# The first product of layer 1 in seven-product form over pairs of super-tiles, with a planned order

## The chip, the cores and the metric

One core of a Trainium2 chip (trn2) runs the whole kernel. The metric is device time in microseconds (us): 1892.49 us is the median of 8 runs before the change (1891.74 to 1893.44), lower is better. The engines are called PE (TensorE), DVE (VectorE), ACT (ScalarE), POOL (GpSimd) and SP (the queue that issues most DMAs). Each takes its instructions in program order.

## The reference

Four residual layers over `x` of 128 graphs x 64 nodes x 256 features, all in float32. Each layer adds to `x` what a different graph block makes of `h = relu(layernorm(x))`. Layer 0 is two graph convolutions followed by four LSTM passes over windows of 1 to 4 nodes; layer 2 weights three parts of the adjacency; layer 3 is masked attention. The change is in layer 1, which is:

```python
h = jnp.maximum(_layernorm(x, axis=-1), 0.0)
agg = jnp.einsum('nm,bmd->bnd', A_hat, h)             # A_hat: normalised adjacency, 64 x 64
z = agg.reshape(-1, d) @ W1.T + b1                    # the first product: 256 -> 512
h = jax.nn.relu(_batchnorm(z, g1, be1))               # statistics over all 8192 rows
out = _batchnorm(h @ W2.T + b2, g2, be2)              # the second product: 512 -> 256
x = x + out.reshape(b, n, -1)
```

Because of the first batchnorm, all 8192 rows of `z` must exist before the second product can start.

## The kernel before

The 8192 rows are cut into 16 super-tiles of 512 rows (`NS` = 16, `SUP` = 512), each of four blocks of 128 rows (`Q` = 4). Features are held in chunks of 128 partitions: 2 for 256 features (`KC`), 4 for 512 (`HC`). The kernel goes through its stages in order: the graph convolutions (about the first 200 us), the LSTM passes (to about 1217 us), the first product of layer 1 (to about 1364 us), its second product, then layers 2 and 3.

There is no automatic scheduler. In most stages the order on each engine is written by hand: a step is noted with a planned time by `at(t, fn, ...)`, the notes are sorted by that time, and the instructions are issued in the sorted order. The times decide the order alone; the waits between engines come from semaphores. The first product alone is issued in another way: `first_product` is a generator that stops at each `yield`, and `pipelined` takes the next piece of several generators in turn.

What one super-tile s goes through in `first_product`: its `x` is loaded into `xt`; `to_token_major` turns the LSTM result `hT` with eight PE transposes (L229), and DVE adds the two halves onto `xt` (L230); `xt` is stored to `x1d`; `norm_of` makes the layernorm figures on DVE (L193 to L197), with one power on POOL (L196); `normalize_relu` makes `h` on ACT (L203); `aggregate` multiplies with `ahT` on PE (L219, eight products of 128 columns) and DVE copies the two banks into `ag` (L220); then for each of the four output chunks two products of 128x512 (L522) go into one bank, which ACT moves with its bias to `zslot(s, o)` (L524). At last DVE takes the statistics of the four chunks (L527), and `bn_coeffs` turns the statistics of all super-tiles into the coefficients `co1` (L761 to L767), two chunks at a time.

In the trace every matmul of this float32 kernel leaves two PE records, so the 128 products of L522 are 256 records.

The first three super-tiles are begun while the LSTM's last steps still run: `begin` puts pieces of `first_product` into the LSTM's plan. The last LSTM steps contain, in this order of dependence, the gate sums on DVE (L628), gate activations on ACT (L624), the cell updates on POOL (L651), their tanh on ACT (L656) and the last states on DVE, written into `hT` (L576). DVE also makes the sums `tx` for the LSTM's own seven-product form (L568). All PSUM tiles come from one pool of eight banks (`bank`).

The LSTM, the second graph convolution, the second product and a product of layer 3 are already in seven-product form. There a 2x2 block of products (two input chunks by two output chunks, over two row blocks) is done with seven products in place of eight, at the price of sums of weights, sums of inputs, and adds of results. The names are those of the code:

```python
    A11, A12, A21, A22, S1, S2, S4 = range(7)
    S3 = A21
    OF = (None, A11, A12, S4, A22, S1, S2, S3)
```

`weight_sum(w, k)` makes the weight sums S1 to S4 on POOL. `adj3` and `smask` are constants used in layers 2 and 3, made in `adjacency_parts` near the start of the kernel.

## Time and profile before

| | us |
|---|---|
| median of 8 runs | 1892.49 |
| lowest and highest run | 1891.74, 1893.44 |
| the profiled execution's own time | 1891.74 |
| its span, first to last instruction | 1889.9 |
| granted TensorE clock | 1.000 |

How the page and the answers are read: a row of the first part gives an engine's busy time, its share of the span and its number of instructions. A row of the chain of waits gives start, duration and the work that the end of the kernel hung on at that time. A row of the table by stretch gives from:to, its length, then busy time and number of instructions of PE, PE's weight loads (PEld), DVE, ACT and POOL, the granted clock, the DMA share and GB/s. A row of the timeline gives start, duration, engine, line, operation, what it writes and reads, the number of instructions merged, and in brackets how long the engine was idle before it and what ended that. Where rows are merged, the duration covers all of them.

The busiest groups of the first product's stage, from the groups of instructions: L522 on PE 112.3 us in 256 records, L219 31.2 us, L229 17.0 us; L524 on ACT takes 0.67 to 0.69 us for one, L527 on DVE 0.68.

### The profile page before, as it was taken

What the parts mean: (1) busy time and instruction counts of PE and PEld (TensorE: products, weight loads), DVE (VectorE), ACT (ScalarE), POOL (GpSimd) and SP (SyncE); (2) the same over time, 40 slices, a digit from 0 to 9 for tenths busy, and PEclk for the clock granted to TensorE, in tenths of its full rate; (3) what the DMA queues carried; (4) which work ended last, traced back from release to release, by engine and by line L of the source; (5) the groups of instructions that cost most, each with busy time, mean ns of one, the idle gap of its engine ahead of it and who ended that gap; (6) DMA issues with size and microseconds to landing.
All of it is one profiled execution on the core that took longest, in us unless ns stands there. A gap on an engine that the chain in (4) does not pass through costs nothing.

```text
span 1889.9 us, 19675 instructions
## 1 busy us (share of the span) xinstructions
PE 1866.6 (99%) x7112; PEld 1176.6 (62%) x7112; DVE 1127.7 (60%) x2264; ACT 892.2 (47%) x1539; POOL 577.2 (31%) x459
## 2 busy tenths in 40 slices
PE   8999999999999999999999999999999999999999
PEld 7996444444445666665444444565444788888887
DVE  6775777635446345435633333577787776677774
ACT  6775766534435435434533333444475344433442
POOL 4441422533325432422532222311053312211220
PEclk9999999999999999999999999999999999999999
DMA  4110001000001000000000000233200111111100
GB/s 139 57 57 0 1 1 42 3 1 0 1 0 45 1 0 1 1 0 23 0 0 1 1 0 23 89 108 108 83 1 1 45 45 43 37 45 45 46 23 34
DMA packets 49537, 54.32 MB, mean 29 GB/s; under 512 B 3104, under 2 KB 44832, under 8 KB 49440
## 3 DMA queue, kind: packets, MB, share of 16 engines
q1 hardware_dynamic: 48976, 52.87, 8.9%
q8 instruction: 56, 0.92, 0.2%
q10 hardware_dynamic: 464, 0.20, 0.1%
q14 instruction: 41, 0.34, 0.1%
HBM read 36.28 MB, written 16.78 MB: 28 GB/s over the span
## 4 chain that ended last, share of the span: by engine, by line
PE 95%; DVE 3%; ACT 1%; POOL 1%; issue 0%; DMA 0%; SPq 0%; DVEq 0%; POOLq 0%
PE ps L606 34%; PE ps L612 19%; PE ps L1012 8%; PE ps L522 6%; PE ps L842 5%; PE ps L338 3%; PE ps L348 3%; PE ps L1076 3%; PE ps L377 2%; PE ps L1052 2%; PE ps L1000 2%; PE ps L1086 2%; PE ps L219 2%; PE ps L1117 1%; PE ps L229 1%; PE ps L1025 1%
## 5 line engine op out<-in xcount | busy, mean ns | idle before, releaser
L628 DVE TENSOR_TENSOR gate<-gate,ps 128x512 f32<-128x512 f32 (+2 forms) x378 | 224.0, 620 | 448.3 <-PE ps L612 369.0
L606 PE MATMUL ps<-tx,wih 128*128 128x512 f32 (+2 forms) x1008 | 446.8, 542 | 2.7 <-ACT gate L631 1.0
L606 PE MATMUL ps<-hT,wih 128*128 128x512 f32 (+2 forms) x756 | 338.5, 541 | 0.0
L631 ACT COPY gate<-ps 128x512 f32<-128x512 f32 (+2 forms) x252 | 134.5, 534 | 378.1 <-PE ps L612 325.0
L606 PEld LDWEIGHTS ps<-tx,wih 128*128 128x128 f32 x1008 | 190.5, 190 | 193.0 <-issue 130.6
L624 ACT ACTIVATE gate<-gate,lbias 128x512 f32<-128x512 f32 (+2 forms) x252 | 216.7, 860 | 157.9 <-DVE gate L628 157.9
L612 PE MATMUL ps<-h,whh 128*128 128x512 f32 (+2 forms) x576 | 256.6, 527 | 0.0
L606 PEld LDWEIGHTS ps<-hT,wih 128*128 128x128 f32 x756 | 143.6, 190 | 141.6 <-issue 79.4
L612 PE MATMUL ps<-th,whh 128*128 128x512 f32 (+2 forms) x432 | 192.5, 527 | 0.0
L1012 PE MATMUL ps<-wl,ag 128*128 128x256 f32 x768 | 172.1, 380 | 0.0
L612 PEld LDWEIGHTS ps<-h,whh 128*128 128x128 f32 x576 | 109.4, 190 | 100.2 <-issue 76.5
L651 POOL TENSOR_TENSOR gate<-gate 128x1024 f32<-128x1024 f32 (+2 forms) x36 | 71.9, 2019 | 306.7 <-ACT gate L624 306.7
L1012 PEld LDWEIGHTS ps<-wl,ag 128*128 128x128 f32 x768 | 143.4, 190 | 20.2 <-ACT ag L1005 1.8
L651 POOL TENSOR_TENSOR cell<-gate 128x1024 f32<-128x1024 f32 (+2 forms) x36 | 79.4, 2228 | 175.2 <-ACT gate L624 175.2
L612 PEld LDWEIGHTS ps<-th,whh 128*128 128x128 f32 x432 | 82.1, 190 | 75.2 <-issue 57.4
L968 POOL TENSOR_TENSOR ln_rn<-ln_rn,mhalf 128x4 f32<-128x4 f32 (+1 forms) x33 | 32.8, 994 | 300.7 <-DVE ln_rn L967 300.2
L975 ACT ACTIVATE h<-x,ln_rn 128x256 f32<-128x256 f32 x128 | 68.3, 594 | 103.1 <-DVE ln_rn L971 103.1
L522 PE MATMUL ps<-ag,w 128*128 128x512 f32 x256 | 112.3, 592 | 0.0
L651 POOL TENSOR_TENSOR cell<-gate,cell 128x1024 f32<-128x1024 f32 (+2 forms) x32 | 65.2, 2055 | 109.3 <-ACT gate L624 109.3
L631 DVE COPY gate<-ps 128x512 f32<-128x512 f32 (+2 forms) x126 | 78.6, 624 | 20.8 <-PE ps L612 20.8
L656 ACT ACTIVATE gate<-cell 128x1024 f32<-128x1024 f32 (+2 forms) x72 | 68.1, 951 | 29.6 <-POOL cell L651 29.6
L522 PEld LDWEIGHTS ps<-ag,w 128*128 128x128 f32 x256 | 47.6, 190 | 54.5 <-issue 50.9
(212 smaller groups left out, 2800.3 us busy)
## 6 DMA issues: line engine op xcount, KB each, us to landing
xt<-in_x_dram SPq DMA_DIRECT2D x30, 512.0 KB, 4.4
x1d<-xt SPq DMA_DIRECT2D x16, 512.0 KB, 2.9
x<-x1d SPq DMA_DIRECT2D x16, 512.0 KB, 5.1
out_dram<-x SPq DMA_DIRECT2D x15, 512.0 KB, 3.4
wih<-in_WihT_dram SPq DMA_DIRECT2D x16, 256.0 KB, 5.4
whh<-in_WhhT_dram SPq DMA_DIRECT2D x12, 256.0 KB, 5.4
xt<-in_x_dram SPq DMA_DIRECT2D x8, 128.0 KB, 3.6
wl<-in_W_dram SPq DMA_DIRECT2D x3, 256.0 KB, 3.0
```

Source lines behind the costliest of these rows:

```text
L338: nc.tensor.matmul(p_[:, ts(q, P)], v[h][:, q, ts(c, P)], adjT_bd, start=True, stop=True)
L522: nc.tensor.matmul(p_, con["w1"][:, c, ts(o, P)], ag[:, c, :], start=(c == 0), stop=(c == KC - 1))
L606: nc.tensor.matmul(wide(p_[:, :N]), wih[0][:, OF[k], gi, :], x_, start=first_, stop=(j == 0), skip_group_check=True)
L612: nc.tensor.matmul(p_[:, :N], whh[0][:, OF[k], gi, :], h_, start=False, stop=True, skip_group_check=True)
L624: nc.scalar.activation(to, r[bank_][:, :N] if bank_ else to, fn, bias=lbias[:, l, m : m + 1])
L628: nc.vector.tensor_add(slot(n, hc), slot(n, hc), r[bank_][:, :N])
L631: op(slot(n, hc), r[bank_][:, :N])
L651: fn(*((t["G"] if isinstance(t, dict) and "G" in t else st["c"])[:, n, :, : st["N"]] for t in tiles))
L656: nc.scalar.activation(o_, c, AF.Tanh)
L842: nc.tensor.matmul(banks[name], w2[:, OF[j], k, :], x_, start=(new and k == 0), stop=(k == 1), skip_group_check=True)
L975: nc.scalar.activation(v[tag][:, q, :], v[src][:, q, :], AF.Relu, bias=v["rn"][:, 1, q : q + 1], scale=v["rn"][:, 0, q : q + 1])
L1012: nc.tensor.matmul(v["W"][:, q, :], v["ag"][:, c, m, ts(2 * k + q, P)], wl2[m][:, c, :], start=(n == 0), stop=(n == 3 * KC - 1))
```

## The change

The first product gets the seven-product form, over pairs of super-tiles and pairs of output chunks: for each pair `i` of super-tiles and each half `g` of the 512 outputs, `half(i, g)` issues seven products of 128x512, which collect in three banks named a, b and c. Bank a takes four products, and is read after each of them; b takes two and is read after each; c takes one. A read is an eviction with bias on ACT (`evict`) or an add onto `z` on DVE (`add`). The fourth product of bank a is issued in the next half.

The generator is replaced by a class `First`, whose steps are issued from a planned list with a period of `GATE` = 8.7 for each half. In it the turned LSTM result is copied from PSUM to `h` by ACT and added onto `xt` by POOL (`turned`, `added`), POOL multiplies the layernorm shift (`root`), and ACT copies the aggregated banks to `ag` (`agged`). The three sums T1, T2, T4 of inputs, and a fourth made in place of `b12`, are `ag_sums`: on POOL, except for the first and the last pair, which have them on DVE. Four super-tiles are begun in the LSTM's last steps, a fifth is loaded there.

PSUM pools are now opened and closed by `new_banks`: eight banks as one pool, but in the first product's loop five for its products ("gates") and three for turns and aggregations ("rest"). The sums of the LSTM's second state, of layer 1 and of layer 3 share one tile (`sums_of`). `adj3` and `smask` are made in a passing tile `parts`, stored to DRAM, and loaded again after the first product; `w1` lies in another pool, with four loads and with weight sums on POOL; the weight sums of `w2` move to the front of the loop.

```diff
-    psum = ctx.enter_context(tc.tile_pool(name="psum", bufs=8, space=bass.MemoryType.PSUM))
...
     graph_weights, first = other_end("first", 1)
-    def bank():
-        return psum.tile([P, 512], F32, tag="ps", name="ps")
+    banks = {}
+    def new_banks(**n):
+        for scope, _ in reversed(list(banks.values())):
+            scope.close()
+        banks.clear()
+        for name, bufs in n.items():
+            scope = ExitStack()
+            banks[name] = scope, scope.enter_context(tc.tile_pool(
+                name=name, bufs=bufs, space=bass.MemoryType.PSUM, reuse_waits="tile"))
+    def bank(pool="psum"):
+        return banks[pool][1].tile([P, 512], F32, tag="ps", name="ps")
+    new_banks(psum=8)
...
-        con["w1"] = weight("w1", a["W1T"])
+        con["w1"] = hlast.tile([P, 7, 2, P], F32, tag="w1", name="w1")
+        for o in range(2):
+            for c in range(2):
+                nc.sync.dma_start(con["w1"][:, 2 * o + c], a["W1T"].rearrange(
...
-    adj3 = const.tile([P, 3, P], F32, tag="adj3", name="adj3")
-    smask = const.tile([P, P], F32, tag="smask", name="smask")
+    parts = first.tile([P, 4, P], F32, tag="parts", name="parts")
+    parts_d = dram.tile([P, 4, P], F32, tag="parts_d", name="parts_d")
...
+        nc.sync.dma_start(parts_d, parts)
...
-            if s == 9:
+            if s in (9, 12):
                 for k in range(4):
-                    at(1.4 + 1.3 * k, lambda k=k: weight_sum(wih0[0], k))
+                    at(1.4 + 1.3 * k, lambda k=k: weight_sum(wih0[0] if s == 9 else con["w1"], k))
...
-    def first_product(s):
...
+    firsts = [{} for _ in range(NS)]
...
+    class First:
+        def __init__(self, s, pool="psum"):
+            self.s, self.v, self.pool = s, firsts[s], pool
+        def load(self):
+            self.v["xt"] = pb[0].tile([P, Q, D], F32, tag="xt", name="xt")
+            nc.sync.dma_start(self.v["xt"], x_r[self.s])
+        def turn(self, k):
+            v = self.v
+            if k == 0:
+                v["h"] = pb[0].tile([P, Q, D], F32, tag="h", name="h")
+            v["T", k] = bank(self.pool).rearrange("p (q d) -> p q d", q=2)
+            for q in range(2):
+                for c in range(KC):
+                    nc.tensor.transpose(v["T", k][:, q, ts(c, P)], tile_rows(self.s, c, 2 * k + q), ident)
+        def turned(self, k, direct=False):
+            v, qs = self.v, slice(2 * k, 2 * k + 2)
+            if direct:
+                nc.vector.tensor_add(v["xt"][:, qs], v["xt"][:, qs], v["T", k])
+            else:
+                nc.scalar.copy(v["h"][:, qs], v["T", k])
+        def added(self, k):
+            v, qs = self.v, slice(2 * k, 2 * k + 2)
+            nc.gpsimd.tensor_add(v["xt"][:, qs], v["xt"][:, qs], v["h"][:, qs])
+        def store(self):
+            nc.sync.dma_start(x1d[self.s], self.v["xt"])
+        def stats(self, q):
+            v = self.v
+            if q == 0:
+                v["st"] = lns.tile([P, Q, 6], F32, tag="ln_st", name="ln_st")
+                v["mv"] = lns.tile([P, Q, 2], F32, tag="ln_mv", name="ln_mv")
+                v["rn"] = lns.tile([P, 2, Q], F32, tag="ln_rn", name="ln_rn")
+            nc.vector.bn_stats(v["st"][:, q, :], v["xt"][:, q, :])
+            nc.vector.bn_aggr(v["mv"][:, q, :], v["st"][:, q, :])
+        def root(self):
+            v = self.v
+            nc.vector.tensor_scalar_add(v["rn"][:, 0, :], v["mv"][:, :, 1], EPS)
+            nc.vector.tensor_scalar_mul(v["rn"][:, 1, :], v["mv"][:, :, 0], -1.0)
+            nc.gpsimd.tensor_tensor(v["rn"][:, 0, :], v["rn"][:, 0, :], mhalf[:, :Q], ALU.pow)
+            nc.gpsimd.tensor_mul(v["rn"][:, 1, :], v["rn"][:, 1, :], v["rn"][:, 0, :])
+        def relu(self, q):
+            v = self.v
+            nc.scalar.activation(v["h"][:, q, :], v["xt"][:, q, :], AF.Relu,
+                                 bias=v["rn"][:, 1, q : q + 1], scale=v["rn"][:, 0, q : q + 1])
+        def agg(self, c):
+            v = self.v
+            if c == 0:
+                v["ag"] = pb[0].tile([P, KC, SUP], F32, tag="ag", name="ag")
+            v["p", c] = bank(self.pool)
+            for q in range(Q):
+                nc.tensor.matmul(v["p", c][:, ts(q, P)], v["h"][:, q, ts(c, P)], ahT,
+                                 start=True, stop=True)
+        def agged(self, c, copy=nc.scalar.copy):
+            copy(self.v["ag"][:, c, :], self.v["p", c])
...
-        t = st["th"] = st["pool"].tile([P, 3, 512], F32, tag="th", name="th")
+        t = st["th"] = (lh0 if st["pool"] is lh0 else sums_of).tile([P, 3, 512], F32, tag="th", name="th")
...
-    def begin(s):
-        early[s] = first_product(s)
-        next(early[s])
+    def ag_sums(i, k, engine=nc.gpsimd):
+        (b11, b21), (b12, b22) = ([firsts[2 * i + n]["ag"][:, c, :] for c in range(KC)]
+                                  for n in range(2))
+        if k == 0:
+            if i == 0:
+                t = sums_of.tile([P, 3, 512], F32, tag="th", name="T")
+                firsts[0]["t"] = [t[:, n, :] for n in range(3)]
+        t1, t2, t4 = firsts[0]["t"]
+        engine.tensor_sub(*((t1, b12, b11), (t2, b22, t1), (b12, b22, b12), (t4, b21, t2))[k])
+    def begin(s, t_load, t_turn=None, t_stats=None, t_relu=None, t_agg=None):
+        f = First(s)
+        def turned():
+            for k in range(2):
+                f.turn(k)
+                f.turned(k, True)
+            f.store()
+        def stats():
+            for q in range(Q):
+                f.stats(q)
+            f.root()
+        def relus():
+            for q in range(Q):
+                f.relu(q)
+        def aggs():
+            for c in range(KC):
+                f.agg(c)
+                f.agged(c, nc.vector.tensor_copy)
+        for when, fn in ((t_load, f.load), (t_turn, turned), (t_stats, stats), (t_relu, relus), (t_agg, aggs)):
+            if when:
+                at(t + when, fn)
     at(t + 8.4, make_room)
-    for s, times in enumerate(((10.5, 12.5, 16.5, 28.3), (11.5, 22.3, 26.2, 31), (13, 33, 36.5))):
-        at(t + times[0], begin, s)
-        for when in times[1:]:
-            at(t + when, lambda s: next(early[s]), s)
+    begin(0, 10.5, 12.5, 12.6, 16.5, 28.3)
+    begin(1, 11.5, 18.8, 18.9, 22.7, 30)
+    begin(2, 13, 22.9, 23.0, 27.2)
+    begin(3, 17, 30.6, 36.1)
+    begin(4, 23)
+    for k in range(4):
+        at(t + 35.3 + 0.1 * k, ag_sums, 0, k, nc.vector)
...
-        gens = [*early, *(first_product(s) for s in range(3, NS))]
-        next(gens[3])
-        next(gens[0])
-        pipelined(gens[4:], 1, gens[3::-1])
+        for k in range(4):
+            weight_sum(w2, k)
+        new_banks(gates=5, rest=3)
+        GATE = 8.7
+        events = []
+        def at(t, fn, *args):
+            events.append((t, len(events), fn, args))
+        def half(i, g):
+            t0, r = GATE * (2 * i + g), {}
+            z = {(n, o): zslot(2 * i + n, 2 * g + o) for n in range(2) for o in range(2)}
+            def product(name, j):
+                new = name not in r
+                if new:
+                    r[name] = bank("gates")
+                (b11, b21), (b12, b22) = ([firsts[2 * i + n]["ag"][:, c, :] for c in range(KC)]
+                                          for n in range(2))
+                t1, t2, t4 = firsts[0]["t"]
+                x_ = (b11, b21, b22, t4, t1, t2, b12)[j - 1]
+                nc.tensor.matmul(r[name], con["w1"][:, OF[j], g, :], x_, start=new,
+                                 stop=(name, j) in (("a", 4), ("b", 3), ("c", 2)), skip_group_check=True)
+            def evict(n, o, name):
+                m = 2 * g + o
+                nc.scalar.activation(z[n, o], r[name], AF.Identity, bias=con["bn1"][:, 0, m : m + 1])
+            def add(n, o, name):
+                nc.vector.tensor_add(z[n, o], z[n, o], r[name])
+            def stats(n, o):
+                nc.vector.bn_stats(st1[:, 2 * g + o, 2 * i + n, :], z[n, o])
+            for t, name, j in ((0, "c", 2), (1.72, "a", 1), (3.46, "b", 5), (4.32, "a", 6),
+                               (6.07, "b", 3), (6.93, "a", 7), (GATE + 0.86, "a", 4)):
+                at(t0 + t, product, name, j)
+            for t, fn, n, o, name in ((2.75, evict, 0, 0, "a"), (3.5, add, 0, 0, "c"),
+                                      (4.5, evict, 1, 1, "b"), (5.35, evict, 1, 0, "a"),
+                                      (7.1, add, 1, 0, "b"), (7.95, add, 1, 1, "a"),
+                                      (GATE + 1.9, evict, 0, 1, "a")):
+                at(t0 + t, fn, n, o, name)
+            for t, n, o in ((5.5, 0, 0), (9.0, 1, 0), (9.7, 1, 1), (GATE + 2.9, 0, 1)):
+                at(t0 + t, stats, n, o)
+            if i == NS // 2 - 1:
+                at(t0 + GATE + 3, bn_coeffs, lns, co1, st1, 2 * g, 2 * g + 2, con["bn1"], "bn1")
+        for i in range(NS // 2):
+            for g in range(2):
+                half(i, g)
+            for k, t in enumerate((-4.3, 0.9, 2.2, 3.5) if i else ()):
+                at(GATE * 2 * i + t, ag_sums, i, k, nc.vector if i == NS // 2 - 1 else nc.gpsimd)
+        for s in range(2, NS):
+            f, t0 = First(s, "rest"), GATE * s
+            for c in range(KC):
+                at(t0 - 2 * GATE + (2.58, 7.8)[c], f.agg, c)
+                at(t0 - 2 * GATE + (3.6, 8.8)[c], f.agged, c)
+            t2 = t0 - 3 * GATE
+            for q in range(Q if s > 2 else 0):
+                at(t2 + 7.1 + 0.6 * q, f.relu, q)
+            if s <= 3:
+                continue
+            if s > 4:
+                at(t0 - 6 * GATE + 9.2, f.load)
+            t1 = t0 - 4 * GATE
+            for k in range(2):
+                at(t1 + 5.19 + 0.02 * k, f.turn, k)
+                at(t1 + 6.3 + 0.6 * k, f.turned, k)
+                at(t1 + 7.0 + 1.3 * k, f.added, k)
+            at(t1 + 8.3, f.store)
+            for q in range(Q):
+                at(t2 + (1.7, 2.3, 4.2, 4.8)[q], f.stats, q)
+            at(t2 + 5.4, f.root)
+        for _, _, fn, args in sorted(events, key=lambda e: e[:2]):
+            fn(*args)
+        new_banks(psum=8)
...
+        adj4 = load_const("adj4", parts_d, [P, 4, P], late)
+        adj3, smask = adj4[:, 0:3, :], adj4[:, 3, :]
...
-                    v["t"] = pc1.tile([P, 5, HALF], F32, tag="tq", name="tq")
+                    v["t"] = sums_of.tile([P, 3, 512], F32, tag="th", name="tq").rearrange(
+                        "p k (n c) -> p (k n) c", c=HALF)
```

## The prediction

> **What bounds the kernel now.** I read, in this order: the share of each engine over the span; the chain of waits in the stage that changes; a table by stretch for one of its periods; what TensorE (PE) waited for; then single instructions at both edges of the stage.

> ```profile
> PE 1866.6 (99%) x7112; PEld 1176.6 (62%) x7112; DVE 1127.7 (60%) x2264; ACT 892.2 (47%) x1539; POOL 577.2 (31%) x459
> ...
> 1322.58 6.87 PE ps L522 x16
> 1329.45 0.90 PE ps L229 x8
> 1330.35 1.79 PE ps L219 x16
> ...
> 1265.25:1274.81 9.56, 9.56 (x42) 5.73 (x41) 7.20 (x19) 4.48 (x8) 1.02 (x1) 1.00 0.35 111
> ```

> PE has no gap in the stage: each super-tile costs 6.87 us of first products (L522), 0.90 of turning (L229), 1.79 of aggregation (L219), 9.56 together, and the stretch of 9.56 us is all PE. VectorE (DVE) fills 7.20 of it, ScalarE (ACT) 4.48, GpSimd (POOL) 1.02. A 128x512 product is two records: 6.87 / 8 = 0.859 us. PE work taken out here shortens the span, as long as the three others keep up.

> The edges of the stage are other regimes:

> ```profile
> 1213.88 4.71 POOL L651 TENSOR_TENSOR cell<-cell,gate 128x1024 f32<-128x1024 f32 x2
> 1218.86 1.04 ACT L656 ACTIVATE gate<-cell 128x1024 f32<-128x1024 f32 x1
> 1220.40 2.49 DVE L576 TENSOR_TENSOR hT<-gate 128x512 f32<-128x512 f32 x4
> ...
> 1364.51 1.28 DVE L527 BATCH_NORM_STATS2 st<-z 128x6 f32<-128x512 f32 x2
> 1365.71 1.01 DVE L761 BATCH_NORM_AGGREGATE bn1mv<-st 128x2 f32<-128x96 f32 x2
> 1367.01 0.70 POOL L764 TENSOR_TENSOR co<-co,mhalf 128x2 f32<-128x2 f32 x1 [3.00 <-DVE co L763]
> 1368.13 0.16 DVE L767 TENSOR_TENSOR co<-bn,co 128x2 f32<-128x2 f32 x1
> ```

> In front, the LSTM's last cell updates run on POOL until 1218.6, their tanh on ACT until 1219.9, the last states on DVE until 1222.9, all under L522 products that started at 1217.47 and wait for none of it. Behind, DVE forms the BatchNorm coefficients: 2.5 us from the last statistics (1365.7) to L767, PE idle beside it.

> [...]

> ```profile
> 1163.40 4.67 POOL L651 TENSOR_TENSOR cell<-cell,gate 128x1024 f32<-128x1024 f32 x2
> ...
> 1167.20 1.41 DVE L568 TENSOR_TENSOR tx<-hT 128x512 f32<-128x512 f32 x1
> 1169.17 0.69 DVE L568 TENSOR_TENSOR tx<-hT,tx 128x512 f32<-128x512 f32 x1 [0.56 <-PE ps L606]
> ...
> 1394.37 1.27 POOL L826 TENSOR_TENSOR T<-z,z 128x512 f32<-128x512 f32 x1 [3.62 <-ACT z L818]
> ...
> 1394.41 0.69 DVE L855 BATCH_NORM_STATS2 st<-hS 128x6 f32<-128x512 f32 x1
> 1395.01 0.68 DVE L855 BATCH_NORM_STATS2 st<-hT 128x6 f32<-128x512 f32 x1
> ```

> The same DVE subtraction takes 1.41 us against a POOL multiply, 0.69 beside an idle POOL; statistics (one SBUF input) and a POOL subtraction pass each other unhurt. [...] the trace has 1.27, which I use. [...]

> **The change part by part.**

> *Products.* 128 become 7 of 8, 112 (8 pairs x 2 halves x 7). 16 x 0.859 = 13.74 us off PE. Turns and aggregations stay. A half is now 7 x 0.859 + 0.90 + 1.79 = 8.70 us.

> *Steady state, each engine per half of 8.70.* DVE: 3 adds, 4 statistics at 0.60, 4 layer-norm pairs at 0.53, two small steps 0.35: 6.65. It gives up the sums onto xt (to POOL) and the ag copies (to ACT). ACT: 4 evictions at 0.57, 4 copies at 0.55, 4 relus at 0.50: 6.5. POOL: even half 3 sums and 2 adds at 1.22 pitch, a root at 1.01 and a small multiply of about 0.2 (from the slope of the L284 rows): 7.3; odd half 4.9. None exceeds 8.70, and DVE's adds and statistics have one SBUF input, so POOL runs at 1.27.

> New waits: bank a is read by ACT or DVE between its products. a1 ends 0.86 us before a6 wants the bank, with a 0.67 eviction between; a7 and the delayed a4 have about as much. ACT starts 0.05 us after PE in this trace (1352.05 to 1352.10). Behind such a wait stands all of PE. I take 0; 0.3 us a half is the other end.

> *Edge in front.* PE does turn 3 before the loop, so it begins near 1217.47 + 0.90 = 1218.4. In the new order ACT does relu(2), 4 x 0.50, ahead of the f gate's last activation (1208.50 before, now 1210.6), so the four cell updates on POOL (9.35 us) run until 1220.65 instead of 1218.6. Tanh follows, and behind it on ACT the first eviction: done 1222.6, a6 was due 1221.8: 0.8 us of stall. Worse is DVE: the four sums T of pair 0 have two SBUF inputs, and wait for the last LSTM product (their tile) and then for POOL's lock: 1220.65 to 1223.1. In order behind them stand layer-norm 3 (2.6), the four last states (2.5), an add, a statistic and two adds (2.5): 1230.7. The states meet POOL's root(3) and the w2 sums, both reading SBUF: between 0 and 2.7 us more; I take 1.2, so 1231.9. The last of those adds frees bank a for a4, due at 1218.4 + 7.8 + 0.86 = 1227.07. Loss in front, which contains the 0.8: 4.8 us; ends 2.7 (T slips in before the lock, states unhurt) and 6.4. The products that once covered these states no longer do, because PE now waits for an add behind them.

> *Edge behind.* The coefficients of channels 0 and 1 are computed in the last half, on DVE ahead of that half's adds: statistics end 24.85 us after the twelfth half began, plus 2.5, then add c, a statistic, add b, add a to 29.95. PE is through a7 at 27.7 and can't issue the last a4 before 30.0: 2.3 us (ends 1.8 and 3). What follows is the old tail: eviction, statistic, 2.5 us, relu.

> *The rest.* w2's four loads go behind x1d(3)'s store in SP's queue and its four sums (0.73 each) ahead of POOL's first xt add: added(4) ends 2 us later than otherwise, against over 5 us until relu(4) is needed; 0. At the start w1 is four loads for one (about 1.5 us more issue), and the store of parts waits for POOL (14.6), so xt(3) is issued at 15.1 instead of 11.4 and lands about 4.1 later, 19.3; its statistics slip from 17.1, the add behind them (21.55) by some 0.3, PE reads that at 27.45: 0, at most 0.5. w1's sums, 2.9 us of POOL, lie in a stage where POOL is busy 53.76 of 140 us: 0. The reload of parts and the later loads at the stage's end are wanted over 100 us later: 0. Other stages keep their order on PE.

> Sum: 13.74 - 4.8 - 2.3 = 6.6 us. Span 1889.9 to 1883.3; that run took 1891.74, 1.84 around the span, so 1885.1; the median, 1892.49, lies 0.75 above it, so 1885.9.

> **The rivals.**

> A, the above: 1885.9, own range 1883 to 1889.5. 58%.

> B, cheap edges: T gets in between two cell updates and the last states find POOL idle, front 1.3, behind 1.8: 1892.49 - 10.6 = 1881.9. For it: POOL's gaps between instructions exist; against it: cell updates follow at once in 1213.88. 18%.

> C, a small stall in each half: ACT's order ties the eviction behind the relus that wait for POOL's root, and DVE's small scale steps can be held by a POOL sum (0.4 us in odd halves). 0.3 x 14 = 4.2 on top: 1890.1, no difference. Against it: 0.9 us of slack. 14%.

> D, slower: POOL becomes the bound. A pair has 8 two-input operations and two roots, 8d + 2.8 us against PE's 17.40. It decides from d = 1.83. If the DVE adds took the lock, d would go to about 2.3: 21.2 a pair, 3.8 over six pairs = 22.8, 1908.7. Break-even with before is d = 1.96. For it: L830 on POOL takes 1.72 in the second product, where DVE has two SBUF inputs; against it, the 1.27 beside statistics, and 2.33 per 1024 beside L628's adds from PSUM. 10%.

> That the product count doesn't fall is no rival: the built order has 112.

> **How the numbers follow.** 0.2% is 3.8 us, about what can be told from no change. Faster (below 1888.7): most of A, all of B, a part of C, 0.78. Same: A's upper end and most of C, 0.12. Slower: D, 0.10. The range leaves out D and the far ends: 1880 to 1891.

> **What would show it.** Right: about 224 records of first products, a period of 8.70 us in the middle, PE waiting for a DVE add once near 1228 to 1232 and once at the last a4, POOL sums at 1.27. Wrong: PE waits in every half on an ACT eviction (C), POOL sums near 1.7 or above (D), no wait at the edges (B), or a new wait in the first 40 us.

## The result, and the profile after

| | before | after |
|---|---|---|
| median | 1892.42 us (31 runs) | 1886.66 us (11 runs) |
| lowest and highest | 1890.98, 1893.59 | 1884.84, 1887.15 |
| profiled execution, its span | 1891.74, 1889.9 | 1887.15, 1885.2 |
| granted clock in that execution | 1.000 | 0.997 |

The ratio is 0.9969, with a 95% interval of 0.9961 to 0.9976. 5.8 us were saved, where 13.7 us of products are gone. The profiled executions stand 4.7 us apart by their spans; the one of after is the longest of its runs. It is the one taken apart below.

First the share of each engine, from the page of after:

```profile
PE 1859.8 (99%) x7080; PEld 1171.4 (62%) x7080; DVE 1137.2 (60%) x2268; ACT 923.7 (49%) x1591; POOL 643.6 (34%) x527
```

PE has 32 records fewer than before (7112), two for each of 16 products. The busy time of POOL is up by 66 us, that of ACT by 31.5. The chain of waits shows the steady part of the stage (start, duration, what). L905 is the product, L585 the aggregation, L541 the turn:

```profile
1249.06 2.58 PE ps L905 x6
1251.64 0.89 PE ps L585 x8
1252.53 1.72 PE ps L905 x4
1254.25 0.90 PE ps L541 x8
1255.15 1.72 PE ps L905 x4
1256.87 0.89 PE ps L585 x8
1257.76 2.58 PE ps L905 x6
```

From 1249.06 to 1257.76 is one half: 14 records of products, 8.70 us, no gap. The table by stretch for a pair (PE, PEld, DVE, ACT, POOL, clock):

```profile
1249.06:1266.46 17.40, 17.40 (x78) 10.70 (x77) 14.09 (x35) 13.79 (x24) 12.34 (x13) 1.00 0.38 122
```

PE is full, the three others have 3.3 to 5.1 us of room in the pair. The loss is at the edges. What PE waited for, from the waits of after (total, times, longest):

```profile
PE ps L905 <- DVE hS L913: 2.5, 1, 2.5
PE ps L905 <- DVE z L913: 1.9, 1, 1.9
...
PE ps L905 <- ACT hS L910: 0.2, 1, 0.2
```

The first is the delayed a4 in front (a4 is product number 4 of the seven, the last that goes into bank a), the second the last a4 of the stage. The timeline around the first:

```profile
1215.96 4.69 POOL L710 TENSOR_TENSOR cell<-cell,gate 128x1024 f32<-128x1024 f32 x2
...
1218.63 2.56 DVE L810 TENSOR_TENSOR T<-ag 128x512 f32<-128x512 f32 x1 [1.18 <-PE ps L671]
...
1225.51 2.49 DVE L635 TENSOR_TENSOR hT<-gate 128x512 f32<-128x512 f32 x4
...
1227.07 1.02 PE L905 MATMUL ps<-ag,w 128*128 128x512 f32 x2
...
1229.24 1.27 DVE L913 TENSOR_TENSOR hS<-hS,ps 128x512 f32<-128x512 f32 x2
...
1230.57 2.03 PE L905 MATMUL ps<-T,w 128*128 128x512 f32 x2 [2.47 <-DVE hS L913]
1232.39 1.86 PE L905 MATMUL ps<-ag,w 128*128 128x512 f32 x2
1234.08 1.05 PE L585 MATMUL ps<-ahT,h 128*128 128x128 f32 x8
```

POOL's last cell updates end at 1220.65; the first sum T, dispatched at 1218.63, gets through only after that, at 1221.19, and takes 2.56 us instead of 0.69. This delay is what the prediction calls POOL's lock; the traces show its length for these operations, not what makes it. Layer-norm 3, the last states and the adds follow in DVE's order, and a4 starts at 1230.57. Then comes what was not expected: from 1230.57 to 1234.08 four records of products take 3.51 us. Elsewhere four take 1.72. The table by stretch of these 3.5 us tells why, in the third column from the end, the granted clock:

```profile
1230.50:1234.00 3.50, 3.43 (x4) 1.47 (x5) 2.96 (x8) 0.69 (x1) 2.71 (x3) 0.52 0.00 0
```

PE ran at half its clock there. The trace's record of the granted clock has three such stretches, from 1230.65, 1360.36 and 1466.17, each of 3.41 us at 0.50, each beside or behind waits of PE (2.47 us until 1230.57, 1.48 until 1360.77, 1.77 until 1465.71). The profiled run of before has none until the program's end.

### The profile page after: what moved, and what is told of

Same layout as the page of the kernel before. It is cut to its first block, busy times and chain, and to the rows that moved or that the text cites. A ratio compares the mean times of both kernels' runs of the same rounds, so it can differ in the third digit from the quotient of the medians.

```text
span 1885.2 us, 19823 instructions
## 1 busy us (share of the span) xinstructions
PE 1859.8 (99%) x7080; PEld 1171.4 (62%) x7080; DVE 1137.2 (60%) x2268; ACT 923.7 (49%) x1591; POOL 643.6 (34%) x527
## 4 chain that ended last, share of the span: by engine, by line
PE 94%; DVE 3%; ACT 1%; POOL 1%; issue 0%; DMA 0%; SPq 0%; DVEq 0%; POOLq 0%
PE ps L665 34%; PE ps L671 19%; PE ps L1185 8%; PE ps L1015 5%; PE ps L905 5%; PE ps L357 3%; PE ps L367 3%; PE ps L1250 3%; PE ps L396 2%; PE ps L1226 2%; PE ps L1173 2%; PE ps L1260 2%; PE ps L1291 1%; PE ps L585 1%; PE ps L1198 1%; PE ps L541 1%
## 5 line engine op out<-in xcount | busy, mean ns | idle before, releaser
L683 ACT ACTIVATE gate<-ps,lbias 128x512 f32<-128x512 f32 (+2 forms) x126 | 79.5, 631 | 3.8 <-PE ps L671 1.0
L627 DVE TENSOR_TENSOR tx<-hT,tx 128x512 f32<-128x512 f32 (+2 forms) x72 | 59.1, 821 | 14.9 <-PE ps L665 10.2
```

Source lines behind the costliest of these rows:

```text
L627: yield nc.vector.tensor_sub(t[k], *((b[1][0], b[0][0]), (b[1][1], t[0]), (b[1][1], b[1][0]), (b[0][1], t[1 % len(t)]))[k])
L683: nc.scalar.activation(to, r[bank_][:, :N] if bank_ else to, fn, bias=lbias[:, l, m : m + 1])
```

## The experiments

### Is the slow stretch the price of standing idle?

Product c of the second half comes just before a4. It is issued three times into its bank, each time starting afresh, so that PE works in the gap.

```diff
+                for _ in range(2 if (i, g, name) == (0, 1, "c") else 0):
+                    nc.tensor.matmul(r[name], con["w1"][:, OF[j], g, :], x_, start=True,
+                                     stop=True, skip_group_check=True)
```

> Two more products are put in front of the first delayed a4: product c of the second half is issued three times into the same bank, each restarting it, so the result is the same and PE has 2 x 0.86 = 1.72 us more work, all of it in the 2.6 us where PE waits for the add behind the last states. Theory (the clock follows the idle time): the four records behind the wait took 3.51 us instead of 1.72 because PE had stood idle for most of a stretch of 3.4 us and the granted clock went to half; with PE busy the clock stays at 1.00 there, a4 still starts near 1230.5, and the span falls by 1.8 us, from 1885.2 to about 1883.4, the time to about 1885.0. Rival (the slow records are slowed by DVE's adds and the weight sums on GpSimd beside them, or by the start behind a wait): the four records still take 3.5 us and the time stays at 1886.7, or rises by up to 1.7.

Measured (x1): 1885.46 us (1884.75 to 1886.65), ratio to before 0.9965 [0.9952, 0.9977], span 1883.6. In the timeline:

```profile
1228.87 1.02 PE L908 MATMUL ps<-ag,w 128*128 128x512 f32 x2
1230.64 1.13 PE L908 MATMUL ps<-T,w 128*128 128x512 f32 x2 [0.75 <-DVE hS L916]
1231.60 1.02 PE L908 MATMUL ps<-ag,w 128*128 128x512 f32 x2
1232.46 1.06 PE L585 MATMUL ps<-ahT,h 128*128 128x128 f32 x8
```

a4 starts at the same time, 1230.64, and the four records behind it take 1.82 us, though DVE's statistics and GpSimd's sums lie beside them as before (from 1230.60 to 1234.00 DVE is busy 3.02 us and GpSimd 2.69, where the 3.50 us of after have 2.96 and 2.71). So neither these nor the start behind a wait make the records slow. That the extra products kept the clock up is not shown by this run, though. The one-pool run below (x6) has the same wait of 2.48 us, no extra products, and no slow stretch behind it. The median falls by 1.2, but the intervals of the two kernels overlap. And the changed kernel itself varies: of its twelve executions whose clock is recorded, six have 0.997 and spans of 1884.8 to 1885.2, the six others 0.998 or 0.999 and 1882.9 to 1884.2. So not every execution pays.

What idle time does is better read from all the traces together. The slow stretches of after last 3.413 us each and start whole multiples of that apart (the figures are in the last section), so a grid of windows of 3.413 us can be laid through each trace. The first line below is the window ahead of the slow stretch in after; the next two are those that share the wait in x6; the last is the one with the wait in x1 (length, then PE; the clock is third from the end):

```profile
1227.24:1230.65 3.41, 0.94 (x3) 0.11 (x2) 3.38 (x7) 2.56 (x5) 3.33 (x5) 1.00 0.00 0
...
1225.99:1229.40 3.41, 2.57 (x12) 1.27 (x10) 3.38 (x8) 1.43 (x3) 3.16 (x4) 1.00 0.00 0
1229.40:1232.81 3.41, 1.77 (x4) 0.87 (x5) 3.09 (x6) 1.73 (x4) 3.41 (x5) 1.00 0.00 0
...
1228.95:1232.36 3.41, 2.66 (x7) 0.98 (x6) 3.10 (x6) 1.73 (x4) 3.41 (x5) 1.00 0.00 0
```

Only the first, with PE busy 0.94 us of 3.41, is followed by half clock. In x6 the same wait is shared by two windows, and both are more than half full. In x1 the window would have held some 1.72 us without the extra products (an estimate: a4 starts at 1230.64 and PE works on to 1232.36), about as much as the 1.77 in x6, so this execution was no test of them. Over the 13 traces of this case, as far as their clock is recorded, every window that PE's records fill to 0.35 or less is followed by half clock; of those between 0.41 and 0.49 seven are and five are not; and no full-clock window above 0.5 is. In after the three ahead of slow stretches are filled to 0.28, 0.33 and 0.44. The slow clock goes with idle windows; no run changes the idle time alone against a fixed grid.

### The chain in front

In the changed kernel relu(2), the four relus of super-tile 2, stands on ACT ahead of the f gate's last activation.

```diff
-    begin(2, 13, 22.9, 23.0, 27.2)
+    begin(2, 13, 22.9, 23.0, 26.5)
```

> relu(2) goes on ACT ahead of the output gate's copy (due time 27.2 to 26.5) into a free stretch of 2.3 us, so the f gate's last activation is no longer behind it. Theory (the chain of the prediction: f activation, cell updates, their lock on the sums T, last states, adds, a4): cell updates end near 1218.8 instead of 1220.65, the first sum T takes under 0.9 us instead of 2.56, the adds end near 1228.7 instead of 1230.5, PE waits about 1.2 us instead of 2.6, too little to halve the clock; span down by 1.8 + 1.8 = 3.6 us, to about 1881.6, time about 1883.2. If the clock still drops: 1.8 less, about 1884.9. Rival (DVE's order alone sets a4, the lock is a side show): cell updates earlier, a4 at 1230 all the same, time 1886.7.

Measured (x2): 1883.66 us (1883.04 to 1884.77), ratio 0.9956 [0.9942, 0.9970], span 1881.7. The timeline:

```profile
1214.69 4.69 POOL L710 TENSOR_TENSOR cell<-cell,gate 128x1024 f32<-128x1024 f32 x2
...
1219.15 0.79 DVE L810 TENSOR_TENSOR T<-ag 128x512 f32<-128x512 f32 x1 [1.18 <-PE ps L671]
...
1224.26 2.49 DVE L635 TENSOR_TENSOR hT<-gate 128x512 f32<-128x512 f32 x4
...
1226.78 1.02 PE L905 MATMUL ps<-ag,w 128*128 128x512 f32 x2
...
1227.99 1.27 DVE L913 TENSOR_TENSOR hS<-hS,ps 128x512 f32<-128x512 f32 x2
...
1229.31 1.12 PE L905 MATMUL ps<-T,w 128*128 128x512 f32 x2 [1.51 <-DVE hS L913]
1230.28 1.02 PE L905 MATMUL ps<-ag,w 128*128 128x512 f32 x2
```

This run's LSTM ended 0.5 us later than that of after. Cell updates end at 1219.4, the sum T passes in 0.79 (it ends 0.56 us after them, where in after it ends 0.54 us after them), states and adds follow earlier, the wait is 1.51 in place of 2.47, and the clock keeps full. The a6 wait of 0.2 is gone too. The chain from relu(2) over the delayed sum T to a4 is shown by undoing its first link. The kernel gains 3.0 us by the medians, 3.5 by the profiled runs. The earlier start of a4 is 1.8 of that (1230.57 against 1229.31, with the 0.5 allowed for); the rest between these two executions is the slow stretches, of which x2's has none.

### The edge behind

The coefficients of channels 0 and 1 go behind the last half's three adds.

```diff
-                at(t0 + GATE + 3, bn_coeffs, lns, co1, st1, 2 * g, 2 * g + 2, con["bn1"], "bn1")
+                at(t0 + GATE + (3 if g else GATE + 0.2), bn_coeffs, lns, co1, st1, 2 * g, 2 * g + 2, con["bn1"], "bn1")
```

> The coefficients of channels 0 and 1 are computed behind the last three adds of the last half instead of ahead of them. Theory: the last a4 waits only for a7 and one add, near 1356.95 instead of 1358.17, and all behind it comes 1.2 us earlier: span 1884.0, time about 1885.4. Rival (the tail is bound by the coefficients, which only change places): the first relus of the second product wait for the moved coefficients, and the time stays at 1886.7 or rises by up to 1.

Measured (x3): 1886.75 us (1885.94 to 1888.59), ratio 0.9972 [0.9962, 0.9983]: nothing gained. In the timeline:

```profile
1354.88 2.07 PE L905 MATMUL ps<-ag,w 128*128 128x512 f32 x4
...
1357.72 1.13 PE L905 MATMUL ps<-T,w 128*128 128x512 f32 x2 [0.78 <-DVE z L913]
...
1360.10 1.87 DVE L916 BATCH_NORM_STATS2 st<-z 128x6 f32<-128x512 f32 x3
...
1361.89 1.01 DVE L857 BATCH_NORM_AGGREGATE bn1mv<-st 128x2 f32<-128x96 f32 x2
```

The last a4 does come earlier: 2.84 us after the pair of products before it started, where after has 3.92. But three statistics now stand behind the coefficients, and the second coefficients start behind them, at 1361.89. Ahead of the last a4 that run stood 0.63 us later than after (1354.88 against 1354.25), whose second coefficients follow the last statistic at 1360.66, so this is 0.6 later. The wait of PE was real, and with a part of it gone the coefficients on DVE, which come later, bound the end.

### Is there anything besides the number of products?

The new plan, pools and loads with the old eight products, each bank evicted once, no sums T, no adds. The weight sum S3 is written over one of the four blocks, which these products use as it is, so one block of the product differs; the work doesn't.

```diff
-        GATE = 8.7
+        GATE = 9.56
...
+            for k, (n, o) in enumerate(((0, 0), (1, 0), (0, 1), (1, 1))):
+                for c in range(KC):
+                    at(t0 + ((0, 0.86), (1.72, 3.46), (4.32, 6.07), (6.93, 8.7))[k][c], product, n, o, c)
+                at(t0 + (1.8, 4.4, 7.0, 9.65)[k], evict, n, o)
+                at(t0 + (2.6, 5.2, 7.8, 10.4)[k], stats, n, o)
```

> The new plan with the old form: eight products in each half (128 in all), each bank evicted once by ACT, no adds, no sums T, period 9.56; all else as in the changed kernel. Theory (the product count is the whole gain and the edges are the whole loss): no wait at either edge, the stage is 16 x 0.859 = 13.74 us of products longer and free of the 8.5 us of waits and slow clock, first relu of the second product near 1368.5, span about 1890, time about 1892.3, no different from before. Rival (the planned order, the five and three banks or the loads moved to the start give or take something of their own): off that by more than 1.5 us either way.

Measured (x4): 1894.75 us (1894.14 to 1896.35), ratio 1.0014 [1.0008, 1.0021], 2.4 above the expectation: by its own terms the rival. Its timeline shows where, in one pair:

```profile
1236.89 0.69 DVE L906 BATCH_NORM_STATS2 st<-z 128x6 f32<-128x512 f32 x1 [3.61 <-ACT z L903]
1237.51 0.15 DVE L569 TENSOR_SCALAR ln_rn<-ln_mv 128x4 f32<-128x4 f32 x1
...
1239.07 1.59 ACT L576 ACTIVATE h<-xt,ln_rn 128x256 f32<-128x256 f32 x3 [0.65 <-POOL ln_rn L572]
...
1240.76 1.41 PE L585 MATMUL ps<-ahT,h 128*128 128x128 f32 x8
1242.00 1.88 PE L898 MATMUL ps<-ag,w 128*128 128x512 f32 x4
```

The layer-norm root stands on DVE behind a statistic that waits 3.61 us for an eviction; the relus follow late, and the aggregation that reads them takes 1.24 us to the next product instead of 0.89. That is a fault of the control's stretched timetable. It was mended by one due time (5.2 to 5.5 in the last line of the diff):

> The eight products in the new plan once more, with one due time of that control moved: the statistic of the second evicted bank goes behind the layer-norm root on DVE (5.2 to 5.5), because in x4 DVE stood 3.6 us behind an eviction with the root queued after it, so relus and aggregations came late by 0.44 us in each of six pairs, 2.6 us. As in x4 the weight block that the sums overwrite is used as it is, so the results of one block differ from the reference; the work is the same. Theory (those waits were the control's own, and the plan without the seven products is worth nothing): 1894.75 - 2.6 = 1892.2, as the kernel before. Rival (the plan, the pools or the early loads cost something of their own): it stays above 1893.5.

Measured (x11): 1892.48 us (1892.0 to 1893.03), ratio 1.0001 [0.9992, 1.0010]. In its trace no aggregation takes more than 0.98 us to the next product, where six of x4 took 1.24 or 1.25. With eight products the plan is neither faster nor slower than the kernel before. The gain goes with the product count; what else was moved gives or takes less than about 2 us in sum (the interval is -1.5 to +1.9 us), and parts that cancel each other within it are not told apart.

### Are two pools of banks needed?

```diff
-        new_banks(gates=5, rest=3)
...
-                    r[name] = bank("gates")
+                    r[name] = bank()
...
-            f, t0 = First(s, "rest"), GATE * s
+            f, t0 = First(s), GATE * s
```

> One pool of eight banks in the first product's loop in place of five and three. Theory: eight banks taken in turn hold each bank for at least as many steps, except that a product bank waits in turn behind the banks of turns and aggregations; no wait in the middle, time 1886.7 within 1.5. Rival (the split is needed): a bank still being read comes up for a turn or an aggregation, PE waits some 0.3 us in every half, 4 us or more slower.

Measured (x6): 1885.87 us (1885.15 to 1887.68), ratio 0.9969 [0.9958, 0.9980], as the changed kernel. PE's waits in the stage are those of the changed kernel, 2.5, 1.9 and 0.2 us, so none of the eight banks comes up too soon. This run's timeline also holds the counter-example to "the wait costs a slow stretch":

```profile
1231.04 1.12 PE L905 MATMUL ps<-T,w 128*128 128x512 f32 x2 [2.48 <-DVE hS L913]
1232.00 1.02 PE L905 MATMUL ps<-ag,w 128*128 128x512 f32 x2
1232.86 1.05 PE L585 MATMUL ps<-ahT,h 128*128 128x128 f32 x8
```

Four records in 1.82 us, with the same a4 behind the same add.

### What GpSimd carries, and how much more it could

All sums T and all sums onto xt on DVE:

```diff
-                at(GATE * 2 * i + t, ag_sums, i, k, nc.vector if i == NS // 2 - 1 else nc.gpsimd)
+                at(GATE * 2 * i + t, ag_sums, i, k, nc.vector)
...
-            nc.gpsimd.tensor_add(v["xt"][:, qs], v["xt"][:, qs], v["h"][:, qs])
+            nc.vector.tensor_add(v["xt"][:, qs], v["xt"][:, qs], v["h"][:, qs])
```

> The sums T and the sums onto xt, which GpSimd makes in six of eight pairs, all go to DVE. By its pitches (adds 0.63, statistics 0.60, layer-norm pairs 0.53, sums 0.61) DVE then has 13.5 + 8 x 0.61 = 18.4 us in a pair of 17.40. Theory (DVE would become the bound; the sums on GpSimd are what lets the shorter products count): 1.0 us a pair over six pairs, 6 us slower than the changed kernel, about 1893, and more (to 1896) if the order on DVE holds the adds up. Rival (DVE's room is larger than its pitches say, or the lock by GpSimd is what costs): 1886.7 or less.

Measured (x7): 1891.13 us (1889.24 to 1891.5), ratio 0.9992 [0.9984, 1.0001]: 4.5 above the changed kernel. One pair in the table by stretch, and below it what PE waited for:

```profile
1267.43:1285.54 18.11, 17.67 (x79) 10.62 (x77) 17.62 (x43) 13.42 (x24) 2.42 (x5) 1.00 0.35 117
```

```profile
PE ps L905 <- DVE hT L913: 2.3, 5, 0.6
```

DVE is busy 17.62 us of a pair that has grown to 18.11. It is the bound, with 0.7 us a pair; the pitches had said 1.0. Without GpSimd four fifths of the saving would be gone. The other way, three sums on GpSimd made twice:

```diff
-        engine.tensor_sub(*((t1, b12, b11), (t2, b22, t1), (b12, b22, b12), (t4, b21, t2))[k])
+        for _ in range(2 if engine is nc.gpsimd and k != 2 else 1):
+            engine.tensor_sub(*((t1, b12, b11), (t2, b22, t1), (b12, b22, b12), (t4, b21, t2))[k])
```

> Three of the four sums T on GpSimd are made twice (same result): 3.8 us more in a pair, 12.3 + 3.8 = 16.1 of 17.40. Theory (GpSimd is under its bound by 5 us a pair and no wait ends on it): within 1.5 us of 1886.7, with single waits below 0.5 us where a doubled sum stands ahead of a root. Rival D of the prediction in a weaker form (GpSimd's order, not its sum, decides): the roots and the sums onto xt come late, PE waits for relus or sums T in every pair, 0.5 us a pair or more, 3 us slower or more.

Measured (x8): 1891.85 us (1890.47 to 1894.72), ratio 0.9999 [0.9991, 1.0008], 5.2 above the changed kernel: the theory missed. A pair in the table, and the waits:

```profile
1260.87:1279.14 18.27, 17.77 (x79) 10.57 (x77) 14.96 (x35) 13.03 (x25) 16.09 (x16) 1.00 0.36 115
```

```profile
PE ps L906 <- POOL T L811: 2.9, 6, 0.5
```

GpSimd is busy 16.09 of 18.27, as summed, and not full. Yet PE waits for a sum T once a pair, 0.5 us and what follows it. T2 stands behind two sums onto xt and is wanted early in the pair; doubled, it is late. The room of 5 us in the pair is room in a sum, not at that place in the queue.

### Mending the edges

On top of the early relu(2): half of the last states on GpSimd, and in the last half add c put into DVE's wait for the power, its statistic behind the last add.

```diff
-                nc.vector.tensor_mul(cols(st["blk"][n], c, st["p"], j),
+                engine = nc.gpsimd if n and st.get("final") else nc.vector
+                engine.tensor_mul(cols(st["blk"][n], c, st["p"], j),
...
+                coeffs = bn_coeffs(lns, co1, st1, 2 * g, 2 * g + 2, con["bn1"], "bn1")
+                for t in (3, 3.6):
+                    at(t0 + GATE + t, next, coeffs)
```

> On top of the early relu(2): the second half of the last states (n = 1) goes to GpSimd, idle there from 1219.4 to 1224.4; and in the last half the add of bank c is put into DVE's wait for the power of the coefficients of channels 0 and 1, and the statistic behind it goes behind the last add. Theory: the front a4 comes 1.2 us earlier (two states of 0.62 less on DVE), the last a4 1.2 us earlier and the coefficients of channels 2 and 3 about 0.9 earlier: span 1881.7 - 1.2 - 0.9 = 1879.6, time about 1881.6. Rival: DVE's chain of 2.5 us of coefficients and four statistics bounds the end whatever the order, as the run with the late coefficients hinted, and only the front gains: time about 1882.5; or the states on GpSimd lock the sums T and nothing is gained in front: 1883.7.

Measured (x5): 1883.16 us (1882.94 to 1883.18), ratio 0.9952 [0.9940, 0.9965], only 0.5 better than x2. From its timeline:

```profile
1226.36 2.50 POOL L636 TENSOR_TENSOR hT<-gate 128x512 f32<-128x512 f32 x2
...
1228.41 1.12 PE L909 MATMUL ps<-T,w 128*128 128x512 f32 x2 [0.30 <-DVE hS L917]
...
1231.67 2.50 POOL L553 TENSOR_TENSOR xt<-xt,h 128x512 f32<-128x512 f32 x2
...
1232.97 0.43 DVE L564 BATCH_NORM_STATS2 ln_st<-xt 128x6 f32<-128x256 f32 x1 [3.42 <-POOL xt L553]
...
1238.49 1.13 PE L909 MATMUL ps<-T,w 128*128 128x512 f32 x2 [1.12 <-DVE z L917]
```

The front a4 waits 0.30 us. But the states run on GpSimd behind the root (the power and the multiply of layer-norm 3), push the w2 sums and the sums onto xt back by some 2 us, DVE waits 3.42 us for these with its adds behind, and the next half's a4 waits 1.12. The w2 sums aren't needed there:

```diff
-        for k in range(4):
-            weight_sum(w2, k)
...
+        for k in range(4):
+            at(GATE * 3 + 1 + 0.01 * k, weight_sum, w2, k)
```

> On top of x5: the four weight sums of w2 leave GpSimd's queue at the front (2.9 us) and go into the free stretch of the fourth half. In x5 two last states of 2.5 us on GpSimd stood ahead of them and pushed the sums onto xt by 2.2 us, DVE waited for those with an add behind them in its order, and PE waited 1.28 us for that add in the second half. Theory: with the weight sums gone that wait goes and nothing else moves: span 1881.0 - 1.3 = 1879.7, time about 1881.9. Rival (the second half's add is late for another reason, the layer-norm order on DVE or the states themselves): 1883.2, no change.

Measured (x9): 1881.58 us (1881.32 to 1881.93), ratio 0.9945 [0.9931, 0.9958]: that wait is gone, 1.6 us by the medians, 1.1 by the median spans. This is the fastest version, 5.1 us below the changed kernel by the medians, 4.5 when each is set against the kernel before as measured beside it.

Last, the order in the four halves without turns, where small delays had been read in the trace of after (up to 0.19 us at a time, 1.2 in all):

```diff
+            late = i >= NS // 2 - 2
-            for t, name, j in ((0, "c", 2), (1.72, "a", 1), (3.46, "b", 5), (4.32, "a", 6),
+            for t, name, j in ((4.32 if late else 0, "c", 2), (0 if late else 1.72, "a", 1),
+                               (1.72 if late else 3.46, "b", 5), (3.46 if late else 4.32, "a", 6),
```

> On top of x9: in the last four halves, which have no turns, product c moves from the front of the half to a place between a6 and b3, so that two products or more stand between the two products of one bank that an ACT or DVE read separates (a1 and a6, a6 and a7, b5 and b3). Theory (in those halves one product of 0.86 us is too little cover for a read: the second product starts 0.96 after the one between, 0.08 to 0.19 late each time, 1.2 us over the four halves): these waits go, span 1.0 to 1.2 us shorter than x9's, time about 1880.8. Rival (the delays come from something else in those halves, or DVE's order at the end takes the gain back): 1881.9 or more.

Measured (x10): 1881.93 us (1881.41 to 1882.34), ratio 0.9947 [0.9934, 0.9959]: no gain. The delays of the last three halves shrank from 0.9 to 0.6 us, but PE waited 0.57 us at one new place, and for the last add 1.50 us in place of 0.78. In x9 and x10 alike the last thing that PE waits for in the stage is an add of DVE.

## Why the prediction was right, and what was mis-sized

It gave 1885.9 within 1880 to 1891, likeliest case A; measured 1886.66. Its sum was 6.6 us for the profiled execution, and 4.7 came. The medians differ by 5.8 because the profiled run of after is the longest of its group and that of before among the shorter. That the sum came so near is in part luck, as the front edge shows.

- *Products*, 13.74 us: right. The period is 8.70; with eight products the plan takes as long as before (x11).
- *Steady state*, no stall, GpSimd operations at 1.27: right. The busy times of a pair, 14.1, 13.8 and 12.3 us, compare with 13.3, 13.0 and 12.2 in the prediction. Rival D fell; x8 shows how near it stood, though: not the sum but the place of one operation in the queue.
- *Edge in front*, 4.8 us: 5.2 in the trace, but not the same 5.2. The chain was the predicted one, shown by x2: relu(2), cell updates until 1220.65, the first T held until 1221.19, the four until 1223.1, states, adds. The states met no contention (2.49 us for the four, as in the kernel before); instead the root on POOL gave way (1.46 us for 1.01). So a4 started at 1230.57, where 1231.9 was predicted, and PE waited 3.4 us in all: 2.64 before a4, and 0.8 at the aggregation, at a6 and behind it. The other 1.8 us are the slow clock, which the prediction didn't have. It took the place of the 1.2 us of contention that did not come: the two errors cancel, and that 4.8 and 5.2 agree is luck.
- *Edge behind*, 2.3 us: 3.4. The wait for the last adds behind the coefficients is 2.2 (3.92 less 1.72), as predicted, and x3 shows its cause. The term that was mis-sized is the small one, the new waits on banks, costed at 0. In the halves with turns it is 0. In the four without, a single product stands between two uses of a bank, and the delays there come to 1.2 us in all, 0.3 a half: the other end that the prediction named for this term. It is not rival C's cause: ACT stands waiting for PE before each of its evictions there (0.17 us and more), and not behind relus. That the single product is too little cover is in part argued: x10 put more between and shrank the delays of three halves by a third.
- *The rest*, 0: 0.6. The clock dropped to half once more from 1466.17, behind a wait of 1.77 us that the trace of before has too, with no slow stretch behind it. The lead of after over before fell from 5.06 us (the turns at 1465.71 and 1470.77) to 4.46 (the products of layer 2 at 1471.95 and 1476.41). The moved w2 sums show no wait of PE in the changed kernel, but stood in the way as soon as the edge was tightened (x5, x9).

Together: 13.74 - 5.2 - 3.4 - 0.6 = 4.5, against 4.7 between the spans.

That the second edge is worth its 2.2 us was not so: x3 took 1.1 of the wait away and gained nothing. An order that also shortens DVE's chain does gain there: in x5 the second coefficients came 1.1 us earlier than in x2, counted from the four records ahead of the last a4.

## What to carry to other kernels

When products are taken out of a stage that PE fills, look at the first and the last period: there work of the neighbouring stages, which longer products used to cover, stands in the other engines' queues ahead of what PE now waits for. Before costing such a wait at its own length, ask whether it can leave a window of 3.4 us less than half full for PE, for then a slow stretch may follow (in after, behind 0.94, 1.12 and 1.51 us of PE in 3.41). A free share of an engine is no licence to put work on it: see what stands behind the new work in its queue (x5, x8), and move first what isn't due (x9).

## What the hardware showed that was not expected

A slow stretch isn't always paid. The one from 1360.36 fell on four records that took 3.4 us in after, where PE had to wait for the next relu until 1364.14 anyway. In x2, at full clock, the records behind these four start 3.37 us after them, as in after, so it moved nothing.
